# The first wave's weight bytes laid out on chip, the norm's first guess by integer operations, row tiles in another load order, row halves spread over the first steps

## The chip, the cores and the metric

The kernel runs on one core of one Trainium2 chip. The core has five engines that take their own instruction streams: TensorE (PE, matrix products and transposes), VectorE (DVE), ScalarE (ACT), GpSimd (POOL) and SyncE (SP, which here only issues transfers). ACT and POOL can issue transfers as well. The metric is the time of one execution on the device in microseconds, the median of three runs.

## The reference

The input is x, 2048 tokens of 1024 numbers. Three layers follow, each on a layer norm of x without learned scale, and each added to x:

```
x = x + 0.5 * ffn(layernorm(x))
x = x + s4(layernorm(x))          # a long convolution along the 1024 columns, by FFT in the reference
x = x + 0.5 * ffn(layernorm(x))   # the same weights again

ffn(x):  h   = silu(x @ Wg) * (x @ Wu)      # Wg, Wu: 1024 x 2752
         out = h @ Wd                        # Wd: 2752 x 1024
W[k, n] = scale[k // 128, n] * (w4[k, n] - (z4[k // 128, n] + 1))
```

The weights are stored as 4-bit numbers, eight in an int32 word: word row r holds the weight rows 8r to 8r+7. Scales and zero points belong to groups of 128 rows.

## The kernel before

**Tiles.** Tokens are taken in four blocks of 512 (four row tiles of 128 rows each). The kernel makes eight jobs of them, one per block and feed-forward layer, in the order JOBS; job 0 is block 0 in the first layer. A job is `gate_up` and then `down`. `gate_up` goes through eight waves (WAVES): the columns of Wg and Wu in blocks of 128, three blocks of each in waves 0 to 4, two in the others. A wave has eight steps, one per group of 128 input rows (STEPS), so a step of wave 0 takes one weight tile of 128 x 768 and makes 12 products of 128x512: six units (a unit is 128 columns of gate or of up), each with the low part (f16, tile xTl) and the high part (fp32r, tile xTh) of the normalized, transposed activations. Every unit accumulates in a PSUM bank of its own. Because each group has its own scale, the sum is multiplied between steps by the ratio of neighbouring scales (`scaled`, tile rat), on ACT for even units and mostly on DVE for odd ones; the product of the next step into that bank waits for it. After the last group `gated` makes the hidden tile.

**Weights.** For a wave the packed words are fetched (`fetch`), split into bytes by integer operations on DVE (`split`, `signed_bytes`: two shifts, two additions of the zero points, bit flips), copied to int8 planes (`dequantize`, plane j is weight rows j, j+8, ...), and written to a DRAM tensor of bytes, w_q[w] (`keep_bytes`). From there `load_bytes` loads a tile of 128 rows and `make_weights` casts it to fp32r on POOL (in a few steps of job 0 on ACT). `next_weights` runs ahead of the products: at step i it loads tile i+4 and casts tile i+3. The later jobs read the same w_q. The zero points of all waves are unpacked on DVE (`zero_points_in_pieces`: eight pieces zi, then the table ztab), stored to DRAM (z_dram) and read back spread over rows (`fetch_zeros`).

**The start.** `start` is written out by hand. It fetches the first wave's words (raw) and zero words, issues the four row tiles x_0_t of block 0 alternately on SP and ACT (line 1899), and the scales of the first blocks. `first_split` (line 583 on) makes the bytes of wave 0: the zero table z (DVE, line 360), the two shifts, two additions and a flip. In `dequantize_first` odd planes are copied by POOL and even ones by ACT, and 16 of a plane's 128 rows go by a transfer of 12 KB straight into `first_tile`, the weight tile of step 0; the whole planes are written to w_q[0] by four stores (`keep_first`, on POOL, ACT and SP), and the tiles of steps 1 to 7 are loaded from there. `first_moments` makes mean and variance: tile 1 on ACT (two passes), the others on DVE. The factor 1/sqrt(variance) comes from `guess` (a power on POOL, line 205) and Newton steps on DVE (`deviations`). `first_rows` normalizes rows, even tiles on DVE and odd ones on ACT, in pieces of 128, 384 and 512 columns; `first_turn(c)` transposes 128 columns of all four tiles on PE, takes the high part out of PSUM (ACT) and makes the low part (DVE; for c of 3, 5, 7 POOL splits a copy of ACT's). `keep_warm` gives PE transposes that nobody reads.

**Order.** A planner orders each engine's instructions by its own estimates, unless the code pins them: `in_order_of_writing(f, engines...)` ties the instructions of f on these engines behind the last one written there. All of `start` is pinned on ACT, DVE, SP, PE and POOL (STARTING is ACT, DVE and SP). Later work of the start, such as turns 1 to 7, the scales of further blocks, the splits of waves 1 and on, hangs on hooks of `gate_up`: `at(up, s, f)` calls f before the products of step s, and s + 0.5 in their middle. The products of steps 0 to 5 are pinned on PE; the loads of steps 0 to 7 on SP; the casts on POOL are not pinned.

## Time and profile before

| What | us |
|---|---|
| median of three runs (2031.41 to 2032.62) | 2032.05 |
| the profiled execution's own time | 2031.49 |
| its span, first to last instruction | 2029.6 |
| PE busy, share of the span | 2002.4, 99% |
| DVE, ACT, POOL busy | 1628.9, 1415.6, 1371.5 |
| first product of step 0 | 17.85 |
| first product of step 1 | 23.13 |
| first product of step 8 (second wave) | 47.3 |
| granted TensorE clock, mean | 0.999 |

The profile is one execution. A line of its timeline gives start, length, engine (SPq and ACTq are transfers issued by SP and ACT), source line, operation, what is written and read, how many instructions are merged, and in brackets how long the engine idled just before and what ended that. Busy time of PE counts its transposes too, and a busy PE need not be at its peak, so the number of products in a stretch is read beside it.

### The profile page before, as it was taken

The page shows a single profiled execution, that of the slowest core. Times are in us where ns is not written, and L with a number is a line of the kernel's source. Part 1 is how long each engine was busy: PE and PEld are TensorE (multiplying, and loading weights), DVE is VectorE, ACT ScalarE, POOL GpSimd, SP SyncE. Part 2 cuts the span into 40 slices and gives each one's busy share as a digit, 9 for nine tenths or more (in the row PEclk, how much of TensorE's full clock was granted, in tenths as well). Part 3 has the DMA queues.
Part 4 walks back from the last instruction along what each step waited for, and adds up shares of the span by engine and source line. Part 5 has one row for each costly group of instructions (what it writes and reads, how often), then busy time and mean ns, then how long its engine had stood idle before and what let it go on. Part 6 is the DMA issues. An engine that isn't in the chain of part 4 may idle for free.

```text
span 2029.6 us, 29690 instructions
## 1 busy us (share of the span) xinstructions
PE 2002.4 (99%) x9202; PEld 1372.3 (68%) x9202; DVE 1628.9 (80%) x2710; ACT 1415.6 (70%) x2222; POOL 1371.5 (68%) x1772
## 2 busy tenths in 40 slices
PE   7999999999999999999999999999999999999998
PEld 4556766577766677656866578667686676866576
DVE  8988878868888878887778777887878878777776
ACT  7888787747775577777767776764776647767776
POOL 6978768748765577655976578754686637965542
PEclk9999999999999999999999999999999999999999
DMA  5343422343524237311552126242263331651113
GB/s 166 119 130 110 130 80 60 80 103 94 146 62 101 75 77 192 120 29 35 143 162 85 33 50 172 79 93 83 50 161 94 83 92 38 160 189 34 35 36 103
DMA packets 345965, 197.13 MB, mean 97 GB/s; under 512 B 166989, under 2 KB 323670, under 8 KB 345798
## 3 DMA queue, kind: packets, MB, share of 16 engines
q1 hardware_dynamic: 344350, 192.81, 35.1%
q10 hardware_dynamic: 1320, 1.94, 0.3%
q8 instruction: 75, 1.23, 0.3%
q14 instruction: 92, 0.75, 0.1%
q0 software_dynamic: 128, 0.39, 0.1%
HBM read 127.52 MB, written 48.57 MB: 87 GB/s over the span
## 4 chain that ended last, share of the span: by engine, by line
PE 95%; DVE 3%; ACT 1%; POOL 0%; issue 0%; DMA 0%; ACTq 0%; DVEq 0%
PE pg L855 60%; PE po L955 30%; PE pc L1344 3%; PE pb L1344 1%; DVE pg L815 1%; ACT pg L811 0%; DVE po L815 0%; DVE rawd L629 0%; DVE stats L1848 0%; PE pt L239 0%; POOL q L670 0%; DMA raw<-in_L_ffn_up_qweight_dram 0%; DVE rawd L632 0%; DVE r L224 0%; PE po L985 0%
## 5 line engine op out<-in xcount | busy, mean ns | idle before, releaser
L811 ACT ACTIVATE pg<-pg,rat 128x512 f32<-128x512 f32 x1280 | 806.4, 660 | 382.3 <-PE pg L855 378.4
L815 DVE TENSOR_TENSOR pg<-pg,rat 128x512 f32<-128x512 f32 x1128 | 748.5, 692 | 147.1 <-PE pg L855 138.7
L855 PE MATMUL pg<-xTh,w_up 128*128 128x512 f32 x2752 | 844.4, 435 | 1.9 <-DVE pg L815 0.7
L855 PE MATMUL pg<-xTl,w_up 128*128 128x512 f16 x2752 | 707.6, 381 | 2.4 <-DVE pg L815 2.0
L855 PEld LDWEIGHTS pg<-xTh,w_up 128*128 128x128 f32 x2752 | 518.4, 189 | 166.1 <-ACT pg L811 7.2
L788 POOL CAST w_up<-b 128x768 fp32r<-128x768 int8 (+2 forms) x491 | 375.4, 771 | 353.5 <-PE pg L855 257.0
L811 ACT ACTIVATE po<-po,ratd 128x512 f32<-128x512 f32 x669 | 438.0, 662 | 145.5 <-PE po L955 144.9
L955 PE MATMUL po<-hl,w_down 128*128 128x512 f32 x1340 | 525.1, 393 | 2.0 <-DVE po L815 1.8
L955 PE MATMUL po<-hh,w_down 128*128 128x512 f32 x1340 | 520.3, 390 | 0.0
L815 DVE TENSOR_TENSOR po<-po,ratd 128x512 f32<-128x512 f32 x611 | 423.9, 696 | 113.2 <-PE po L955 112.9
L855 PEld LDWEIGHTS <-w_up 128*128 128x128 bf16 x2752 | 226.9, 98 | 339.6 <-issue 154.4
L788 POOL CAST w_down<-bd 128x512 fp32r<-128x512 int8 x352 | 218.2, 623 | 148.5 <-PE po L955 75.5
L955 PEld LDWEIGHTS po<-hl,w_down 128*128 128x128 f32 x1340 | 251.2, 188 | 63.4 <-DVE po L815 7.2
L955 PEld LDWEIGHTS po<-hh,w_down 128*128 128x128 f32 x1340 | 251.6, 188 | 50.9
L897 POOL TENSOR_TENSOR hl<-hf,hh 128x512 fp32r<-128x512 f32 x168 | 217.0, 1292 | 7.0
L896 POOL CAST hh<-hf 128x512 fp32r<-128x512 f32 x168 | 108.5, 646 | 81.2 <-DVE hf L890 62.4
L890 DVE SCALAR_TENSOR_TENSOR hf<-pg,rat,g 128x512 f32<-128x512 f32 x168 | 120.9, 746 | 38.3 <-ACT g L887 32.6
L887 ACT ACTIVATE g<-pg,rat 128x512 f32<-128x512 f32 x168 | 110.0, 687 | 33.9 <-PE pg L855 17.9
L1029 POOL TENSOR_TENSOR x<-x,yr 128x512 f32<-128x512 f32 x52 | 66.8, 1285 | 0.0
L291 POOL TENSOR_TENSOR lo<-x,hi 128x512 f16<-128x512 f32 x48 | 62.0, 1291 | 0.0
L189 DVE BATCH_NORM_STATS2 stats<-x 128x6 f32<-128x512 f32 x88 | 60.0, 682 | 0.0
L289 POOL TENSOR_TENSOR mid<-hi,top 128x512 bf16<-128x512 f32 x48 | 56.0, 1166 | 0.0
(225 smaller groups left out, 1083.3 us busy)
## 6 DMA issues: line engine op xcount, KB each, us to landing
b<-wq SPq DMA_DIRECT2D x319, 96.0 KB
bd<-wdq SPq DMA_DIRECT2D x336, 64.0 KB
x<-in_L_attn_u_dram SPq DMA_DIRECT2D x30, 512.0 KB
yz<-y SPq DMA_DIRECT2D x56, 256.0 KB
yr<-yz SPq DMA_DIRECT2D x56, 256.0 KB
b<-wq SPq DMA_DIRECT2D x128, 64.0 KB
sz<-xn SPq DMA_DIRECT2D x16, 512.0 KB
st<-sz SPq DMA_DIRECT2D x64, 128.0 KB
```

The costliest lines, as they stand in the source:

```text
L291: nc.gpsimd.tensor_tensor(lo[:, own], n[:, own], hi[:, own].bitcast(F32), ALU.subtract)
L788: nc.gpsimd.tensor_copy(t, b)
L811: nc.scalar.activation(dst, src, AF.Copy, scale=sc)
L815: nc.vector.tensor_tensor(dst, src, sc.to_broadcast(list(dst.shape)), ALU.mult)
L855: product = lambda: nc.tensor.matmul(p, weights, (lo, hi)[k][:, g, :], start=(g == 0 and not done), stop=(g == GK - 1 and done), skip_grou ...
L887: nc.scalar.activation(g, pg, AF.Silu, scale=rat[:, 2 * f, GK - 1 :])
L890: nc.vector.scalar_tensor_tensor(hf, pu, last, g, ALU.mult, ALU.mult)
L896: nc.gpsimd.tensor_copy(hi, hf)
L897: nc.gpsimd.tensor_tensor(lo, hf, hi.bitcast(F32), ALU.subtract)
L955: nc.tensor.matmul(ps[c], w[:, bass.ts(c, P)], part, start=(f == 0 and k == 0), stop=(f == NF - 1), skip_group_check=True,)
L1029: nc.gpsimd.tensor_tensor(part, part, rows_back.pop((a, t)), ALU.add)
L1344: nc.tensor.matmul(dst, lhsT, rhs, start=start, stop=stop, skip_group_check=True)
```

## The change

The words of wave 0 are fetched with their row groups interleaved: partition 8r+g holds word row r of group g (rearranged source; the zero words are spread to match). Then the 128 rows of a plane j are, in order, the rows that belong to partitions j, j+8, ... of the eight weight tiles, and one transfer of 96 KB per plane puts them all into `landed`, 128 partitions x 8 tiles x 768 bytes, which takes the place of the loads of steps 0 to 7. `landed` lies in the pool of the y tiles; it is written to w_q[0] in one transfer at step 3 (`keep_landed`). The bytes of wave 1 no longer use that pool: they go to four half tiles with four stores (`keep_half`), their copies are pinned on ACT, and the loads of tiles 8 and 9 and the cast of tile 8 are put off (LATE) to step 5.5, behind these stores.

The zero table of wave 0 goes from DVE to ACT; the zero words of the other waves are fetched on SP instead of ACT. Row tile 1 is issued first, then 2, 0, 3, and DVE takes tiles 2, 0, 3. `first_deviations` replaces power and Newton steps by an integer first guess and two steps on DVE, ten instructions on 128x4 numbers. The scale work of the first blocks comes after all planes and its reciprocal between the first and second row pieces. The high part of turn 0 is taken out half by DVE, half by ACT. Seven zero pieces stay in `start`, the last three calls move to step 0.5; the second row halves (512 columns) move from `start` to steps 1, 1.5 and 2; turns 2 and 3 move by half a step. Step 0 takes all six high products first and then the six low ones. Further hooks of steps 0 to 9 shift by half a step or more, one rescale at step 4 goes from ACT to DVE, and the rescales of steps 0 to 6 are pinned.

```diff
...
             own = slice(GK * SEG * i, GK * SEG * (i + 1))
-            nc.scalar.dma_start(z[own], src.rearrange("g (s n) -> (g s) n", s=SEG))
+            nc.sync.dma_start(z[own], src.rearrange("g (s n) -> (g s) n", s=SEG))
         return z
...
-    def unpacked_zeros_in_pieces(tab, z, zi):
+    def unpacked_zeros_in_pieces(tab, z, zi, on_act=False):
...
             yield
...
+        if on_act:
+            nc.scalar.activation(dst, src, AF.Copy, bias=120.0 * 257, scale=-8.0 * 257)
+        else:
+            nc.vector.tensor_scalar(dst, src, -8.0 * 257, 120.0 * 257, ALU.mult, ALU.add)
...
-    first_tile = bpool.tile([P, width_of(0)], I8, tag="b", name="b_0_0")
+    landed = ypool.tile([P, 4 * TB], F32, tag="y", name="landed").bitcast(I8)[:, : 8 * width_of(0)]
+    landed = landed.rearrange("p (g n) -> p g n", g=GK)
     minus_128 = const.tile([P, 1], F32, tag="minus_128", name="minus_128")
...
         for own, i, lo, hi in columns(w):
-            queues[i].dma_start(raw[:, own], (gate_qw, up_qw)[i][:, lo:hi])
+            src = (gate_qw, up_qw)[i][:, lo:hi]
+            if w == 0:
+                src = src.rearrange("(g r) n -> r g n", g=GK)
+            queues[i].dma_start(raw[:, own], src)
             yield
...
             src = (gate_qz, up_qz)[i][:, lo // 8 : hi // 8]
-            wide = src.unsqueeze(1).to_broadcast([GK, 16, own.stop - own.start])
+            wide = src.unsqueeze(0).to_broadcast([16, GK, own.stop - own.start])
             queue.dma_start(z[:, own], wide)
...
         raw = packed.pop(0)[0]
-        unpacked_zeros(z, zq, zi)
+        unpacked_zeros(z, zq, zi, True)
         nc.vector.tensor_scalar(even, raw, 3, NIBBLES, ALU.logical_shift_left, ALU.bitwise_and)
...
                 nc.scalar.activation(q, view(even, U8), AF.Identity, bias=minus_128)
-            queue = nc.scalar if j == 6 else nc.sync
-            queue.dma_start(first_tile[j:P:8], q[: P // 8])
-
-        def keep(odd, half, queue):
-            rows = w_q[0].rearrange("(r b a two) n -> two b r a n", b=2, a=2, two=2)[odd, half]
-            queue.dma_start(rows, pairs[odd, half].rearrange("p (a n) -> p a n", a=2))
-
-        return dequantize, keep
+            queue = nc.scalar if j in (2, 6) else nc.sync
+            queue.dma_start(landed[j:P:8], q)
+
+        return dequantize
+
+    def keep_landed():
+        nc.sync.dma_start(w_q[0].rearrange("(g p) n -> p g n", p=P), landed)
+
...
         n = width_of(w)
+        if w == 1:
+            if j % 4 < 2:
+                half = t2(f"q_1_{j}").bitcast(I8)[:, : 2 * n]
...
         if w == 1 and j % 2 == 0:
...
...
+    def keep_half(odd, half):
+        rows = w_q[1].rearrange("(r b a two) n -> two b r a n", b=2, a=2, two=2)[odd, half]
+        nc.sync.dma_start(rows, unpacked.pop((1, odd, half)))
...
             s0 = (0, 4, 8 * w - (14 if w < 5 else 15))[min(w, 3) - 1]
-            steps = (0.5, 1, 2.5, 3, 3) if w == 1 else range(6)
+            steps = (1.5, 2, 3, 3.5, 3.5) if w == 1 else (1, 1.5, 2, 3, 4, 5) if w == 2 else range(6)
             in_pieces(at, [(up, s0 + d) for d in steps], lambda w=w: split(w))
-            copies = {1: (3, 3, 3.5, 3.5) + (3.5,) * 4, 2: (3, 3, 4, 4, 5.5, 5.5, 6, 6)}
+            copies = {1: (3.5, 4, 5, 5.5) + (4,) * 4, 2: (3, 3, 4, 4, 5.5, 5.5, 6, 6)}
             copies = copies.get(w, (3, 3, 4, 5, 6, 6, 7, 8))
...
             for k, d in zip(EVEN_FIRST, copies):
-                at(up, s0 + d, lambda w=w, k=k: dequantize(w, k))
-            for odd, o in enumerate({1: (3.5, 3.5), 2: (5.5, 7)}.get(w, (6.5, 9.5))):
+                make = lambda w=w, k=k: dequantize(w, k)
+                make = lambda w=w, k=k, make=make: in_order_of_writing(make, *STARTING[:1] * (w == 1))
+                at(up, s0 + d, make)
+            if w == 1:
+                for odd, half, s in ((0, 0, 4.5), (1, 0, 4.5), (1, 1, 5), (0, 1, 5.5)):
+                    at(up, s, lambda odd=odd, half=half: keep_half(odd, half))
+                at(up, 5.5, late_weights)
+                continue
+            for odd, o in enumerate({2: (5.5, 7)}.get(w, (6.5, 9.5))):
                 at(up, s0 + o, lambda w=w, odd=odd: keep_bytes(w, odd))
...
         j, stage, s = queue[i]
-        if i == 0:
-            loaded[i] = first_tile
+        if i < GK:
+            loaded[i] = landed[:, i, :]
             return
...
             make_weights(k)
-        if i + LOAD < len(queue):
+        if i + LOAD < len(queue) and i + LOAD not in LATE:
             load_bytes(i + LOAD)
-        if i + MAKE < len(queue):
+        if i + MAKE < len(queue) and i + MAKE != LATE[0]:
             make_weights(i + MAKE)
         return made.pop(i)
+
+    LATE = GK, GK + 1
+
+    def late_weights():
+        for i in LATE:
+            load_bytes(i)
+        make_weights(LATE[0])
...
             if j == s == 0:
-                turns = [(1 - k, pos, done) for k, pos, done in turns]
+                turns = [(1 - k, pos, k == 1) for k in range(2) for pos in range(len(order))]
             for i, (k, pos, done) in enumerate(turns):
-                if i == len(order):
+                if i == len(order) // (1 + (j == s == 0)):
                     for hook in hooks.get(s + 0.5, ()):
...
                     if unit == 2 * fs[0 if n == 3 else 1] + 1:
-                        on_act = (j == 0 and n == 3 and g in ((4, 6) if s < 8 else (0, 4, 6)))
+                        on_act = (j == 0 and n == 3 and g in ((6,) if s < 8 else (0, 4, 6)))
                         on_act = on_act or (j < 2 and g % 2 == 0 and (j or n == 2))
...
                     rescale = lambda: scaled(on_act, p, p, rat[:, unit, g : g + 1])
-                    in_order_of_writing(rescale, *STARTING[:2] * (j == s == 0))
+                    in_order_of_writing(rescale, *STARTING[:2] * (j == 0 and s < 7))
                 elif unit == 2 * WIDE:
...
                 rows = {}
-                for s, f in ((0, lambda: fetch_zeros(1)), (1, lambda: fetch(2)), (2, lambda: fetch_zeros(2))):
+                for s, f in ((1, lambda: fetch_zeros(1)), (1, lambda: fetch(2)), (2, lambda: fetch_zeros(2)), (3, keep_landed)):
                     at(up, s, pinned(f, ET.SP))
-                for first_use, s, k0, k1 in ((4, 0, 3, 9), (6, 1, 9, 15), (30, 11, 15, WIDE)):
+                for first_use, s, k0, k1 in ((3, 0, 3, 9), (5.5, 1, 9, 15), (30, 11, 15, WIDE)):
                     load = lambda k0=k0, k1=k1: rows.update({k0: scale_rows(k0, k1)})
                     at(up, s, lambda load=load: in_order_of_writing(load, ET.SP))
-                    steps = [(up, first_use + i / 2) for i in range(4)]
+                    late = {3: 1.5, 9: 0.5}.get(k0, 0)
+                    steps = [(up, first_use + i / 2 + late * (i > 1)) for i in range(4)]
                     in_pieces(at, steps, lambda k0=k0, k1=k1: scales_in_pieces(k0, k1, rows.pop(k0)))
...
                     more = lambda c=c: first_turn(c)
-                    at(up, {1: 0.5, 2: 0.5, 4: 2.5}.get(c, c - 2), pinned(more, *STARTING, ET.PE))
+                    at(up, {1: 0.5, 2: 1, 3: 1.5, 4: 2.5}.get(c, c - 2), pinned(more, *STARTING, ET.PE))
+                for _ in range(3):
+                    at(up, 0.5, pinned(lambda: next(points, None), ET.Activation, ET.DVE))
+                for t, s in ((0, 1.5), (1, 1), (2, 2), (3, 1.5)):
+                    more = lambda t=t: first_rows(t, 512, HID)
+                    at(up, s, pinned(more, *STARTING))
                 first_weights(up, dn, at)
...
         nc.scalar.activation(scratch, x[0][1], AF.Square, bias=mean, scale=-1.0, accum_out=squares)
-        for t in (0, 2, 3):
+        for t in (2, 0, 3):
             for i in range(2):
...
         return mv, scratch
+
+    def first_deviations(mv):
+
+        tiny = lambda a: small.tile([P, NT], F32, tag=a, name=f"{a}_0_1")
+        ve, r, e = tiny("ve"), tiny("r"), tiny("e")
+        nc.vector.tensor_scalar(ve, mv[:, :, 1], EPS, (256 / (3 * LIFT)) ** 2, ALU.add, ALU.mult)
+        bits = r.bitcast(I32)
+        nc.vector.tensor_scalar(bits, ve.bitcast(I32), 1, -1, ALU.logical_shift_right, ALU.bitwise_and)
+        nc.vector.tensor_scalar(bits, bits, -1.0, float(0x5F3759DF - 2**31), ALU.mult, ALU.add)
+        nc.vector.tensor_tensor(e, r, r, ALU.mult)
+        nc.vector.tensor_tensor(e, e, ve, ALU.mult)
+        nc.vector.scalar_tensor_tensor(r, e, -3.0, r, ALU.add, ALU.mult)
+        nc.vector.tensor_tensor(e, r, r, ALU.mult)
+        nc.vector.tensor_tensor(e, e, ve, ALU.mult)
+        nc.vector.scalar_tensor_tensor(e, e, -40.0 / 3, e, ALU.add, ALU.mult)
+        nc.vector.scalar_tensor_tensor(r, e, 80.0, r, ALU.add, ALU.mult)
+        for t in range(NT):
+            ln[0, t] = (mv[:, t, 0:1], r[:, t : t + 1], 1)
+        return r
...
         ps = bank(f"pt_0_1_{c}")
-        for t in range(NT):
+        for t in (0, 2, 1, 3):
             src = first[t, c // 4][:, bass.ts(c % 4, P)]
             nc.tensor.transpose(ps[:, bass.ts(t, P)], src, ident)
-        if c not in (3, 5, 7):
+        if c == 0:
+            for i, copy in enumerate((nc.vector.tensor_copy, nc.scalar.copy)):
+                view = lambda a: a.rearrange("p (t two n) -> p two t n", two=2, n=P)[:, i]
+                copy(view(hi), view(ps))
+            nc.vector.tensor_tensor(lo, ps, hi.bitcast(F32), ALU.subtract)
+        elif c not in (3, 5, 7):
             nc.scalar.copy(hi, ps)
...
         fetch(0, (nc.sync, nc.scalar))
-        for t, src in enumerate(rows_of(u, 0)):
-            (nc.sync, nc.scalar)[t % 2].dma_start(x[0][t], src)
+        for t, queue in ((1, nc.sync), (2, nc.scalar), (0, nc.sync), (3, nc.scalar)):
+            queue.dma_start(x[0][t], rows_of(u, 0)[t])
         nc.gpsimd.memset(minus_128, -128.0)
...
         zeros_down = zero_words(1)
-        dequantize_first, keep_first = first_split(zq)
+        dequantize_first = first_split(zq)
         second = fetch_in_pieces(1)
-        for j in (1, 3, 5):
+        mv, scratch = first_moments()
+        for j in (1, 0, 3, 2, 5, 7, 4, 6):
             dequantize_first(j)
-        next(second)
-        dequantize_first(7)
-        mv, scratch = first_moments()
-        dequantize_first(0)
+        for _ in second:
+            pass
         first_scales = scales_in_pieces(0, 3, srow)
         next(first_scales)
-        dequantize_first(2)
         next(first_scales)
-        guess(0, 1, mv, LIFT)
-        for _ in range(2):
-            keep_first(1, _, nc.gpsimd)
-        dequantize_first(4)
-        dequantize_first(6)
-        keep_first(0, 1, nc.scalar)
-        keep_first(0, 0, nc.sync)
-        next(second)
-        for _ in first_scales:
-            pass
         keep_warm(10, scratch)
...
         bias = small.tile([P, NT], F32, tag="bias", name="bias")
-        r = deviations(0, 1)
+        r = first_deviations(mv)
+        points = zero_points_in_pieces(0, zeros)
         nc.vector.scalar_tensor_tensor(bias, mv[:, :, 0], -1.0, r, ALU.mult, ALU.mult)
...
             first_rows(t, 0, P)
-        for t in (0, 1, 2):
+        for _ in first_scales:
+            pass
+        for t in (0, 2, 1):
             first_rows(t, P, 512)
-        points = zero_points_in_pieces(0, zeros)
-        for _ in range(4):
+        first_turn(0)
+        first_rows(3, P, 512)
+        for _ in range(7):
             next(points)
-        first_turn(0)
-        for _ in range(5):
-            next(points)
-        first_rows(3, P, 512)
-        for t in range(NT):
-            first_rows(t, 512, HID)
-        for _ in points:
-            pass
         keep_warm(6)
-        return zeros_down
-
-    zeros_down = in_order_of_writing(start, *STARTING, ET.PE, ET.Pool)
+        return zeros_down, points
+
+    zeros_down, points = in_order_of_writing(start, *STARTING, ET.PE, ET.Pool)
     x.pop(0)
...
```

More of the change, by code (lines that the diff above doesn't have):

```diff
@@ L359, in unpacked_zeros_in_pieces @@
             yield
-        nc.vector.tensor_scalar(
-            tab.bitcast(U16).rearrange("p (n k) -> p n k", k=2),
-            zi.unsqueeze(2).to_broadcast([p, 8 * n, 2]),
-            -8.0 * 257,
-            120.0 * 257,
-            ALU.mult,
-            ALU.add,
-        )
+        dst = tab.bitcast(U16).rearrange("p (n k) -> p n k", k=2)
+        src = zi.unsqueeze(2).to_broadcast([p, 8 * n, 2])
+        if on_act:
+            nc.scalar.activation(dst, src, AF.Copy, bias=120.0 * 257, scale=-8.0 * 257)
+        else:
+            nc.vector.tensor_scalar(dst, src, -8.0 * 257, 120.0 * 257, ALU.mult, ALU.add)
     def zero_points(which, z):
@@ L662, in dequantize @@
         n = width_of(w)
-        if w not in unpacked:
-            q = ypool.tile([P, 4 * TB], F32, tag="y", name=f"q_{w}").bitcast(I8)[:, : 8 * n]
-            unpacked[w] = q.rearrange("p (two a n) -> p two a n", two=2, a=4)
-        q, src = unpacked[w][:, j % 2, j // 2, :], packed[w][j % 2][:, j // 2, :]
+        src = packed[w][j % 2][:, j // 2, :]
+        if w == 1:
+            if j % 4 < 2:
+                half = t2(f"q_1_{j}").bitcast(I8)[:, : 2 * n]
+                unpacked[1, j % 2, j // 4] = half.rearrange("p (a n) -> p a n", a=2)
+            q = unpacked[1, j % 2, j // 4][:, j // 2 % 2, :]
+        else:
+            if w not in unpacked:
+                q = ypool.tile([P, 4 * TB], F32, tag="y", name=f"q_{w}").bitcast(I8)[:, : 8 * n]
+                unpacked[w] = q.rearrange("p (two a n) -> p two a n", two=2, a=4)
+            q = unpacked[w][:, j % 2, j // 2, :]
         if w == 1 and j % 2 == 0:
@@ L670, in dequantize @@
             nc.gpsimd.tensor_copy(q, src)
-        if j == 7:
+        if j == (6 if w == 1 else 7):
             packed.pop(w)
```

## The prediction

> **What bounds the kernel now.** First the page: engine shares and the chain that ended last.
>
> ```profile
> span 2029.6 us, 29690 instructions
> PE 2002.4 (99%) x9202; PEld 1372.3 (68%) x9202; DVE 1628.9 (80%) x2710; ACT 1415.6 (70%) x2222; POOL 1371.5 (68%) x1772
> ...
> PE 95%; DVE 3%; ACT 1%; POOL 0%; issue 0%; DMA 0%; ACTq 0%; DVEq 0%
> ```
>
> TensorE is the bound; 27.2 us (2029.6 - 2002.4) is all that it ever idles. The change touches only the start, so the second view is the busy time of each engine in stretches cut at the first product (17.85), the second step (23.13) and the eighth (44.60).
>
> ```profile
> 0.00:17.85 17.85, 5.83 (x34) 5.00 (x34) 13.40 (x38) 9.37 (x16) 9.77 (x22) 1.00 0.57 189
> 17.85:23.13 5.28, 4.39 (x24) 2.97 (x25) 4.48 (x15) 4.67 (x8) 0.92 (x2) 1.00 0.63 202
> 23.13:44.60 21.47, 20.39 (x102) 12.13 (x101) 18.80 (x29) 17.63 (x30) 18.56 (x24) 1.00 0.41 126
> 20.10:44.60 24.50, 22.53 (x113) 13.48 (x112) 21.06 (x32) 20.43 (x35) 19.48 (x25) 1.00 0.44 134
> ```
>
> Columns: stretch, PE, PEld, DVE, ACT, POOL busy, then clock 1.00 and DMA. In 23.13 to 44.60 three helpers are each over 80% busy. After it the chain has 31.95 us for 140 products, 0.228 each, so a step of 12 costs 2.7. Seven steps at 2.7 (18.9), seven turns of activations at 0.44 (3.1) and two groups of scale turns at 0.47 (0.9) make 22.9 us; 17.85 to 44.60 is 26.75. So 3.85 us can be won there, and whatever the first product comes earlier.
>
> Third, the timeline of the start.
>
> ```profile
> 8.55 1.06 ACT L1844 ACTIVATE scratch<-x 128x1024 f32<-128x1024 f32 x1 [3.67 <-DMA x<-in_L_attn_u_dram]
> 13.46 1.04 POOL L205 TENSOR_TENSOR r<-ve,minus_half 128x4 f32<-128x4 f32 x1 [0.42 <-DVE ve L203]
> 14.45 1.72 POOL L613 DMA_DIRECT2D wq<-q  x2
> 16.74 1.35 DVE L351 TENSOR_SCALAR zi<-zq 128x43 int32<-128x43 int32 x4
> 16.94 0.81 POOL L788 CAST w_up<-b 128x768 fp32r<-128x768 int8 x1
> 17.15 0.56 ACT L1880 CAST xTh<-pt 128x512 fp32r<-128x512 f32 x1
> 17.85 0.93 PE L855 MATMUL pg<-xTh,w_up 128*128 128x512 f32 x3 [0.17 <-POOL w_up L788]
> 20.11 1.24 ACT L811 ACTIVATE pg<-pg,rat 128x512 f32<-128x512 f32 x2 [0.38 <-DVE xn L1865]
> 22.21 1.60 POOL L788 CAST w_up<-b 128x768 fp32r<-128x768 int8 x2 [4.45 <-DMA b<-wq]
> 22.64 0.66 PE L1878 MATMUL pt<-ident,xn 128*128 128x128 f32 x4 [0.89 <-DVE xTl L1881]
> 23.10 1.12 DVE L625 TENSOR_SCALAR even<-raw 128x768 int32<-128x768 int32 x1
> ```
>
> POOL stood 4.45 us for the second tile's bytes, yet PE at 22.64 was held by DVE's low half. Both waits end at 23.0 to 23.1, so taking only the bytes' trip away gives nothing.
>
> **The change part by part.** Times are single records of this trace.
>
> *Row tiles.* They land in order of issue at 7.08, 8.52, 9.82 and 10.52. Tile 1 goes first, so ACT's 2.4 us of moments begin at 7.1 instead of 8.55. DVE reads tile 2 (8.52) at 8.95, tile 0 (9.82) at 10.30, tile 3 (10.52) at 11.70: no wait. DVE's line, from the packed words (5.31) through the statistics to 13.2, is the longer one, so by itself this gives 0; it lets ACT finish its even planes by 13.5 (14.4 before), with one more DMA issue (0.54) among them.
>
> *Zero table on ACT.* On DVE it ran 4.39 to 5.35, inside the wait for the words that ended at 5.31: gain 0. On ACT the shape is not shown: between 1.06 (128x1024) and 1.6 (that times 1.5) from 4.87, done by 5.9 to 6.5; DVE needs it at 6.52. I take 0; end +0.1.
>
> *Planes.* Eight transfers of 12 KB become 96 KB; four stores (1.72 us of POOL's issue, 0.73 of ACT's, 0.58 of SP's), three loads and their wait go. SP's issues stay near 0.5 each; its order meets planes ready at 9.6, 10.35, 10.4, 11.2, 11.9, 12.7, so nothing queues long, and the two zero-word DMAs that move to SP fall in its gap before 9.65. A 96 KB load took 2.45 (19.71 to 22.16); the last plane, issued at 13.5 on ACT, lands at 16.0. POOL can cast five tiles straight on, 4 to 5 us earlier than now.
>
> *First guess.* From the variance (13.21) to the bias (15.38) was 2.17, with POOL's 1.04 inside. Now ten dependent DVE instructions at the 0.20 to 0.26 that the Newton steps show: 2.0 to 2.6. I take 2.1, so 0; ends -0.15 and +0.4.
>
> *First product.* The reciprocal (0.45) sat beside POOL's power and now lies between DVE's row pieces. DVE: bias at 15.3, two pieces at 0.25, reciprocal 0.45, two at 0.39, then its half of the first high part, between 0.3 and 0.56 (ACT's whole one): 0.4. High part at 17.5 (17.70 before). POOL: ratios 0.37 and 0.43 after the reciprocal at 16.35, cast 0.82: 17.97 (17.755 before). First product at 18.0, +0.1; if the cast goes before the ratios, 17.5, -0.3.
>
> *First step.* The second row halves leave it. ACT's first rescale stood at 20.11. Now: three products to 18.7, turn 0.44, ACT's copy to 19.8, DVE's low half to 20.45, the last zero piece and the table (0.7) to 21.2, ACT's store of the table, whose issue stands ahead of the rescales, to 21.6. So ACT starts its rescales 1.5 later than before, DVE at 21.2 against 20.43. The seven zero pieces in front take 0.65 (0.09 apart where POOL is idle) and fit DVE's gap from 18.2 to 19.8.
>
> *To the eighth step.* Both helpers' lists: ACT has 20 rescales at 0.57 (11.4), 6 copies at 0.58 (3.5), 2 row halves at 0.71 (1.4), 2 scale copies (0.5), 4 planes at 0.83 (3.3): 20.1, from 21.6 to 41.7. DVE has 19 rescales at 0.60 (11.4), 3 low halves at 0.61 (1.8), 2 row halves at 0.46 (0.9), the next splits (0.56, 0.56, 0.96, 0.96, 0.57 and 0.56, 0.56, 0.96: 5.7), a reciprocal 0.75: 20.6, from 21.2 to 41.8. PE alone would be there at 40.9. With no wait 41.8, -2.8. ACT idled 24.5 - 20.4 = 4.1 in the same stretch before; with all of that, 45.9, +1.3. Two idles have lost their cause: the 1.26 us before 42.99, where POOL's plane copies held back the scales, whose reciprocal now comes 1.5 steps later, and some 0.5 around 23 to 26 that hung on the second tile. 2.3 remain: 44.1, -0.5.
>
> *Second wave's bytes.* The next load is late here if anything is. Tile 8's cast waits for four stores, whose last plane ACT makes in the middle of step 5. From that plane's end: store 2.95 (38.96 to 41.9), load 2.45, cast 0.82, issues 0.2: 6.4. Two and a half steps with a turn and scale turns are 7.2 to 7.7, less about 1 of queue on ACT: slack -0.2 to +0.3. I take 0; end +1. The 768 KB kept at step 3 on SP goes ahead of these stores; the same bytes in four stores took 5.2 (14.45 to 19.65), so it ends before them: 0, and +2 if not.
>
> *After.* From 44.6 the list of work is the same and shifts as a whole: 0, give or take 0.5.
>
> Sum: -0.5. The profiled execution itself took 2031.49 (span 2029.6 and 1.89 around it) and would take 2031.0; it lies 0.56 under the median 2032.05, so the predicted median is 2031.5.
>
> **A rule against the change.** The rows first: one zero piece, issued at 16.74 as POOL's cast began, took 1.079 us where the seven others took 0.19, and the 0.56 shift at 23.10 took 1.12 under casts. At 500.7 two DVE instructions on rows, under four POOL casts, took turns with them, one for one.
>
> [...]
>
> **The rivals.**
> *The lock (slower).* In 17.75 to 22.21, when DVE unpacked zeros, POOL idled; now it casts there. If one zero piece passes per cast, five casts at 0.8 let DVE go at 22.4 instead of 18.85; low half to 23.0, table to 23.8, store to 24.2: first rescale 24.2, not 21.6. That is +2.6 on the sum, less 0.6 of blocking that the later splits no longer meet (the 0.56 at 23.10): +1.5 in all, 2033.5; from +0.5 to +4 (if all idle stays). It decides once three of the seven pieces take over 0.5 each. Against it: small pieces overlap and may pass together.
> *Second wave late (slower).* If tile 8's cast ends after step 7, every step from there waits: +1 to +5, 2035. For it: the slack above. Against: before, the cast ended at 45.98 for a use at 47.3.
> *All stalls gone (faster).* First product at 17.6 and PE unhindered: 17.6 + 22.9 = 40.5, -4.1, 2028; up to -2.8 if the lists bind without idling. Against: three helpers over 80% busy.
> *The bytes were hidden anyway.* The low half at 22.64 says so; then the same idle stays, +1.3 at most; it is the upper end of my case.
>
> **How the numbers follow.** 0.2% is 4.1 us, about what a measurement of this kernel can tell from no change. My case, -2.8 to +1.3 (2029.2 to 2033.4): 0.45. Lock 0.30, second wave late 0.10, all stalls gone 0.15. Faster by over 4.1: half of the last (0.07) and 0.06 for later stretches moving: 0.13. Slower: a third of the lock (0.10), most of the second wave (0.06), 0.03 for the rest: 0.19. Within: 0.68. Range: 2028.2, below which half of the all-gone case lies, to 2036.0, above which lie a tenth of chance of the lock and the second wave.
>
> **What would show it.** ACT's moments at 7.1; no stores of the first wave before step 3; casts two to five right behind the first; POOL without a power; first product at 17.5 to 18.1; first ACT rescale at 21.6 (24.2: the lock, with zero pieces of 0.8); eighth step at 44.1; tile 8's cast ended before it is used. Wrong if DVE's row pieces also stand behind casts before the first product, or if the order on POOL, which only the planner sets, puts ratios or later turns behind five casts.

## The result and the profile after

The changed kernel takes 2035.76 us (median of 14, 2033.57 to 2037.45), the kernel before, run beside it, 2031.99 (2030.86 to 2033.0): a ratio of 1.0019 with a 95% interval of 1.0011 to 1.0026. So it is slower, by about 3.8 us. Its profiled execution took 2035.14, 3.65 more than that of before (2031.49); the two profiles are compared below. The page of the changed kernel:

```profile
span 2033.3 us, 29687 instructions
...
PE 2003.5 (99%) x9202; PEld 1373.6 (68%) x9202; DVE 1631.6 (80%) x2716; ACT 1416.6 (70%) x2222; POOL 1368.9 (67%) x1769
```

PE is busy for 1.1 us more and idle for 29.8 us instead of 27.2. Step starts (first product of each step) show where:

| step | before | after | shift |
|---|---|---|---|
| first | 17.85 | 18.13 | +0.28 |
| second | 23.13 | 24.31 | +1.18 |
| third | 26.48 | 29.06 | +2.58 |
| fourth | 30.10 | 34.33 | +4.23 |
| eighth | 44.61 | 47.65 | +3.04 |
| ninth | 47.30 | 51.46 | +4.16 |
| seventeenth | 69.15 | 73.05 | +3.90 |
| sixty-fourth | 184.10 | 187.77 | +3.67 |

Everything is lost in the first nine steps, and the rest only carries it on. Busy time by stretch of the changed kernel, cut at its first product, second and eighth step (columns as in the prediction):

```profile
0.00:18.13 18.13, 5.86 (x33) 5.06 (x34) 12.65 (x41) 11.02 (x17) 7.04 (x20) 1.00 0.64 211
18.13:24.31 6.18, 3.85 (x21) 2.55 (x22) 6.15 (x14) 1.71 (x4) 3.87 (x5) 1.00 0.05 18
24.31:47.65 23.34, 21.95 (x104) 13.68 (x104) 21.61 (x32) 20.07 (x34) 16.22 (x21) 0.93 0.39 124
```

In the second stretch DVE is busy for 6.15 of 6.18 us (4.48 of 5.28 before), with fewer instructions, and ACT for only 1.71. In the third the granted clock is 0.93, where it was 1.00. The timeline of that second stretch says why DVE has no time:

```profile
17.26 3.92 POOL L808 CAST w_up<-landed 128x768 fp32r<-128x768 int8 x5
...
17.96 0.69 DVE L1935 TENSOR_TENSOR xTl<-pt,xTh 128x512 f16<-128x512 f32 x1 [0.44 <-ACT xTh L1934]
...
18.57 2.93 DVE L351 TENSOR_SCALAR zi<-zq 128x43 int32<-128x43 int32 x7
...
21.40 0.68 DVE L1938 TENSOR_TENSOR xTl<-pt,xTh 128x512 f16<-128x512 f32 x1
...
22.00 0.57 DVE L351 TENSOR_SCALAR zi<-zq 128x43 int32<-128x43 int32 x1
22.60 0.52 DVE L365 TENSOR_SCALAR ztab<-zi 128x688 uint16<-128x688 int32 x1
...
23.15 0.34 ACTq L378 DMA_DIRECT2D z_dram<-ztab  x1
23.59 1.81 ACT L838 ACTIVATE pg<-pg,rat 128x512 f32<-128x512 f32 x3 [3.44 <-DVE ztab L365]
24.31 1.24 PE L882 MATMUL pg<-xTl,w_up 128*128 128x512 f16 x3 [2.32 <-ACT pg L838]
```

Five casts run without a gap, as the change meant them to. Beside them seven zero pieces of 43 elements take 2.93 us: four at 0.19 to 0.35 and three at 0.88, one for each of three casts. DVE's low half of the second turn waits behind the pieces, and behind it the eighth piece and the table. ACT's queue stands 3.44 us at the store of the table, with three rescales behind it. PE, which needs those rescales, stands 2.32.

Then comes a second loss. Clock and busy time of PE in three stretches of 3.41 us around that wait:

```profile
21.13:24.54 3.41, 1.09 (x8) 0.71 (x7) 3.38 (x10) 0.95 (x2) 0.87 (x2) 1.00 0.14 51
24.54:27.96 3.42, 3.42 (x12) 2.57 (x11) 2.39 (x5) 3.42 (x7) 0.00 (x0) 0.50 0.15 46
27.96:31.37 3.41, 3.41 (x22) 2.12 (x21) 2.75 (x5) 2.94 (x5) 1.93 (x3) 1.00 0.81 239
```

PE was busy for 1.09 of 3.41 us, and its clock was halved for the next 3.42: 12 matmuls (8 products and 4 transposes) where the stretch after it has 22 (12 and 10). In the third and fourth step DVE then lost more turns to POOL, as these lines of its timeline show:

```profile
30.03 0.99 DVE L1917 TENSOR_SCALAR xn<-x,mv,r 128x512 f32<-128x512 f32 x1
30.94 1.64 DVE L627 TENSOR_SCALAR raw<-raw 128x768 int32<-128x768 int32 x1
...
37.34 1.52 DVE L634 TENSOR_SCALAR raw<-raw 128x1536 uint16<-128x1536 uint16 x1
```

A row half took 0.99 (0.54 in the kernel before, at 19.52), a shift 1.64 and a bit flip 1.52 (0.55 for the shift at 27.61 and for the flip at 55.1). The ninth step waited 0.95 for the cast of its tile.

### The profile page after: what moved, and what is told of

Read it like the earlier page. It is cut to its first block, busy times and chain, and to the rows that moved or that the text cites. A ratio compares the mean times of both kernels' runs of the same rounds, so it can differ in the third digit from the quotient of the medians.

```text
span 2033.3 us, 29687 instructions
## 1 busy us (share of the span) xinstructions
PE 2003.5 (99%) x9202; PEld 1373.6 (68%) x9202; DVE 1631.6 (80%) x2716; ACT 1416.6 (70%) x2222; POOL 1368.9 (67%) x1769
## 3 DMA queue, kind: packets, MB, share of 16 engines
q8 instruction: 75, 1.23, 0.2%
## 4 chain that ended last, share of the span: by engine, by line
PE 95%; DVE 3%; ACT 1%; issue 0%; DMA 0%; POOL 0%; ACTq 0%; DVEq 0%
PE pg L882 60%; PE po L982 30%; PE pc L1371 3%; PE pb L1371 1%; DVE pg L842 1%; ACT pg L838 0%; DVE po L842 0%; DVE rawd L631 0%; DMA raw<-in_L_ffn_up_qweight_dram 0%; DVE stats L1881 0%; PE pt L239 0%; DVE zi L351 0%; DVE rawd L634 0%; PE po L1012 0%; DVE r L224 0%
## 5 line engine op out<-in xcount | busy, mean ns | idle before, releaser
L808 POOL CAST w_up<-b 128x768 fp32r<-128x768 int8 (+2 forms) x483 | 368.7, 769 | 348.5 <-PE pg L882 257.4
```

The lines of the kernel that those rows point to most:

```text
L808: nc.gpsimd.tensor_copy(t, b)
```

## The experiments

Each kernel's ratio is to the kernel before, timed beside it (medians of 2030.87 to 2031.99), with a 95% interval in brackets. A profile is one execution, and often one of the faster ones: its rows account for that execution, and not for the whole of a median.

**The bytes alone, and one tile alone.** The kernel before, its tiles of the first steps cast from the bytes of the first tile, which lie on the chip at once. The right weights of steps 1 to 7, and their loads, are left out. For the second kernel `i < 2` stands in place of `i < GK`:

```diff
-        if i == 0:
+        if i < GK:
             loaded[i] = first_tile
```

> The kernel before, with one edit: the weight tiles of steps 1 to 7 are cast from the same bytes as that of step 0, so they wait for no trip through DRAM (this leaves the right weights of these steps out of the computation). Theory that the bytes were hidden, plus the lock: POOL casts at 17.7 to 21 instead of 22.2 to 25.6, but DVE's last zero pieces, table and two row halves (18.6 to 20.5) now stand behind casts, so the second step begins 0.3 to 1.5 us later than 23.13, and the kernel is between 1 us faster (POOL's relief later) and 1.5 us slower. Theory that the trip was the stall: the second step at 22.3 or earlier, and 1.5 to 3 us faster than before.

> The kernel before, with the second tile alone cast from the bytes of the first (its weights are wrong in that step), so two casts follow one another at 17.1 instead of five. If a row piece of DVE is starved as long as casts follow without a gap (4.5 with five casts): it takes 2.0 to 2.3 with two, ending at 18.7, and the second step starts at 24.5 to 25 instead of 27.18 with five; eighth step 45 to 46, time 2032 to 2033. If DVE and POOL take turns one for one: the piece takes 1.2 at most, the second step starts at 23.1 as before and the time is 2031.5.

With all tiles: 2035.2 against 2031.48, ratio 1.0020 (1.0010 to 1.0030). The early bytes by themselves cost as much as the whole change. Its timeline:

```profile
15.77 5.44 DVE L1865 TENSOR_SCALAR xn<-x,mv,r 128x128 f32<-128x128 f32 x4
...
17.09 3.90 POOL L788 CAST w_up<-b 128x768 fp32r<-128x768 int8 x5
...
22.22 1.22 PE L855 MATMUL pg<-xTl,w_up 128*128 128x512 f16 x3 [3.29 <-DVE xTl L1881]
```

The last of the four row pieces (128x384) begins at 16.68, before the casts, while POOL works on the scales, and takes 4.54 us; the piece of the same shape ahead of it takes 0.47. It ends 0.2 after the fifth cast, at the first gap in POOL's work since 16.5. The casts keep their 0.81 to 0.82. So it isn't one turn for one. With two casts in a row (2032.7 against 2031.0, ratio 1.0008, 0.9998 to 1.0017):

```profile
16.68 2.13 DVE L351 TENSOR_SCALAR zi<-zq 128x43 int32<-128x43 int32 x4
...
16.88 1.59 POOL L788 CAST w_up<-b 128x768 fp32r<-128x768 int8 x2
...
18.70 0.68 DVE L1881 TENSOR_TENSOR xTl<-pt,xTh 128x512 f16<-128x512 f32 x1
```

Here the first of four zero pieces is the one that waits, 1.87, until the second cast is over. The second step starts at 23.86, less late than the 24.5 that I had expected: the row piece was through before the casts began. By the profiles what is lost grows with the casts in a row: the second step starts at 23.13 before, 23.86 with two and 27.19 with five. The times of the two kernels lie 1.0008 and 1.0020 over before, with intervals that overlap.

**The zero pieces, the store.** Seven pieces between the dependent instructions of the guess, before any cast; and, in another kernel, the table's store issued by SP (with the calls at step 0.5 pinned there as well):

```diff
         nc.vector.tensor_tensor(e, r, r, ALU.mult)
+        next(between, None)
...
-        for _ in range(7):
-            next(points)
```
```diff
-... else (z_dram, SEG, nc.scalar)
+... else (z_dram, SEG, nc.sync)
```

> The changed kernel, with one edit: seven of the eight zero pieces leave their place behind the first low half and stand between the dependent instructions of the norm's first guess on DVE, where POOL makes no cast. Lock theory (three pieces of 0.88 us behind POOL's casts hold the second low half, the table and with it ACT's store): the pieces take 0.2 each, the first product comes up to 0.6 later (18.1 to 18.7), ACT's first rescale goes from 23.6 to about 21.8 and the second step from 24.3 to 22.5 to 22.9; the kernel is 1.5 to 2.0 us faster than the changed one (about 2034.0). Rival theory (the row halves moved into steps 1 and 2 overload ACT and DVE, whenever these start): the second step begins earlier, but the fourth (34.3) moves by less than 0.7 and the time by less than 0.7.

> The changed kernel, with one edit: the store of the zero table is issued by SP instead of ACT, so that ACT's rescales do not stand behind an issue that waits for DVE's table. Lock theory with its second half (the loss reaches PE through ACT's queue): DVE's pieces stay at 0.88, but ACT's idle 3.44 us before 23.6 shrinks to about 1, its first rescale comes at 20.7 to 21.0, and though DVE's first rescale stays at 23.0 the backlog on ACT in steps 1 and 2 is 2.5 us smaller: 1.0 to 2.5 us faster than the changed kernel. If DVE alone carries the loss: second step within 0.5 of 24.3 and under 0.7 us gained.

Early pieces: each takes 0.2, the second low half begins at 20.38 in place of 21.40, the first ACT rescale is at 22.45 and the second step at 23.16, as before the change. But the median is 2035.37, ratio 1.0022 (1.0013 to 1.0032): no gain. In the profiled execution, the fastest of ten (2033.48), PE still stands 0.99, 1.18 and 0.94 at 22.2, 36.0 and 48.1, and the fourth step is at 31.32 (30.10 before); what the slower executions lose isn't shown. Store on SP, by its timeline:

```profile
18.59 2.93 DVE L351 TENSOR_SCALAR zi<-zq 128x43 int32<-128x43 int32 x7
...
20.58 1.82 ACT L838 ACTIVATE pg<-pg,rat 128x512 f32<-128x512 f32 x3 [0.41 <-PE pg L882]
```

The pieces are as slow as ever, but ACT rescales 3 us sooner, and the second step is at 22.24. The time is 2034.25, ratio 1.0015 (1.0006 to 1.0025): off ACT's queue the store leaves the kernel 2.8 above the one before in place of 3.8, a difference that the intervals don't separate. Neither edit alone brings the time back.

**The casts held back.** POOL reads one element before it casts tiles two to five: of the second low half, or (with the store on SP) of the table; in a third kernel, with the pieces early, the store on SP and the order of copies that is tried next, the cast of each tile from the second to the eighth comes behind the low half of the turn before its own. The first kernel's edit, in part:

```diff
...
+    def held_weights():
+        nc.gpsimd.tensor_copy(t, pieces[0][1][:1, 1, :1])
+        for k in range(1, MAKE + 1):
+            make_weights(k)
```

> The changed kernel, with its bytes as early as before, but POOL reads one element of the second turn's low half before it casts the second tile, so casts two to five can't run beside the zero pieces. If the lock between DVE's unpacking and POOL's run of casts is what slows the change: zero pieces of 0.2 to 0.35 instead of 0.88, the second low half at 19.8 to 20.4 instead of 21.40, casts two to five at 20.5 to 24, second step at 23.1 to 23.4 instead of 24.31, eighth step at 45 to 46 instead of 47.65, time 2032 to 2033.5. If the row halves and the store in steps 0 to 2 are what slows it, and the lock only fills idle time: the eighth step stays at 47.4 to 47.8 and the time at 2035 to 2036.

> The changed kernel with casts two to five held until DVE has the table of zero points (one element of it read by POOL), and the table's store on SP, so that neither the lock nor the store stands before ACT's first rescale. Lock and store together as the cause: zero pieces 0.2 to 0.35, first rescale on ACT at 20.2 to 20.7, second step at 22.2 to 22.6, eighth step near the 44.1 of the prediction, time 2030.8 to 2032, no slower than the kernel before. If the row halves in steps 1 and 2 cost as much as they save: eighth step at 45 to 46.5, time 2032.5 to 2034.

> The three edits together (zero pieces early, store on SP, third-wave copies in order), and casts two to eight no longer back to back: POOL reads one element of the low half of a turn before it casts the tile after next to that turn's (tile c+1 behind turn c), so casts come one per turn. If runs of casts without a gap are what the chip punishes: DVE instructions lengthened by under 2 us in all between 15 and 52 us, no PE gap over 0.8 before the ninth step, eighth step at 42.5 to 43.5, and a spread of executions as narrow as that of the kernel before (3 us or less); median 2029 to 2030.5. If the waits put on POOL cost what the lock cost: a cast late for its step (PE waiting for POOL at a step's start), eighth step 44 to 46, median 2031 to 2033.

Held behind the low half: 2034.48 against 2031.0, ratio 1.0015 (1.0005 to 1.0024). Its timeline:

```profile
17.21 0.82 POOL L808 CAST w_up<-landed 128x768 fp32r<-128x768 int8 x1
...
18.57 0.74 DVE L351 TENSOR_SCALAR zi<-zq 128x43 int32<-128x43 int32 x7
...
20.14 0.69 DVE L1945 TENSOR_TENSOR xTl<-pt,xTh 128x512 f16<-128x512 f32 x1 [0.83 <-ACT xTh L1944]
...
20.98 1.23 DVE L365 TENSOR_SCALAR ztab<-zi 128x688 uint16<-128x688 int32 x1
21.02 4.19 POOL L808 CAST w_up<-landed 128x768 fp32r<-128x768 int8 x5
...
23.40 0.95 PE L888 MATMUL pg<-xTl,w_up 128*128 128x512 f16 x3 [1.47 <-ACT pg L844]
```

Without casts beside them the seven pieces take 0.74 in place of 2.93, so the casts are what stretched them; the table, now under a cast, takes 1.23 in place of 0.52. The profiled eighth step is at 45.50 in place of 47.65. Behind the table, with the store on SP: first rescale 20.66, second step 22.70, as expected. Then comes, by its timeline,

```profile
28.00 1.08 DVE L1925 TENSOR_SCALAR xn<-x,mv,r 128x512 f32<-128x512 f32 x1
...
29.13 0.55 PE L1938 MATMUL pt<-ident,xn 128*128 128x128 f32 x3 [1.21 <-DVE xn L1925]
```

the stretching of a row half that the change moved to step 2, from 0.54 to 1.08, and PE waits for it. What runs beside it here is POOL's split of a turn (27.53, 1.26), not a cast. Eighth step 44.89, 2034.07, ratio 1.0013 (1.0004 to 1.0023). Paced: second step 21.87, the same wait of 1.2 at 28.0, eighth step 44.95, 2034.97, ratio 1.0016 (1.0007 to 1.0025), and no wait of PE over 0.5 between the second and the ninth step was ended by a cast. My expectation for it failed both ways: casts no longer ran back to back, none was late for PE, and yet POOL's work met other instructions of DVE. Held casts are not lost casts: they, or the work that they push back, land on something else.

**Third-wave copies behind the casts on POOL**, so that tile 8's cast is not queued behind one:

```diff
-..., *STARTING[:1] * (w == 1))
+..., *STARTING[:1] * (w == 1), *[ET.Pool] * (w == 2))
```

> The changed kernel, with one edit: the third wave's first copies are pinned on POOL behind the casts written before them, so the cast of tile 8 (at 50.58, behind a copy at 49.81) comes first. Second-wave theory: the copy's 0.77 us on POOL is what PE idles 0.95 for at 50.5; the ninth step begins at 50.6 to 50.8 instead of 51.46, and the kernel is 0.7 to 0.9 us faster than the changed one (about 2035.0). If instead the bytes themselves are late (loaded at 49.3), the ninth step moves by less than 0.3.

The changed kernel's timeline around tile 8:

```profile
49.32 0.54 POOL L431 TENSOR_TENSOR rat<-s_gu,safe 128x84 f32<-128x84 f32 x1 [1.69 <-DVE safe L427]
...
49.81 0.82 POOL L679 COPY q<-even 128x768 int8<-128x768 int8 x1
...
50.58 1.60 POOL L808 CAST w_up<-b 128x768 fp32r<-128x768 int8 x2
...
51.46 0.82 PE L882 MATMUL pg<-xTl,w_up 128*128 128x512 f16 x3 [0.95 <-POOL w_up L808]
```

With the copy behind, the cast is at 49.98 and the ninth step at 50.85, 0.61 sooner; by the seventeenth step it is 73.13 against 73.05, and the time is 2036.2, ratio 1.0027 (1.0016 to 1.0037). The ninth step's wait for its cast exists, and taking it away gains nothing that shows here.

**The row halves back in the start; the power back.** The halves are all written in the start again; or POOL's power and the Newton steps are the first guess again, first ahead of the plane copies, then behind them.

```diff
-        r = first_deviations(mv)
+        r = deviations(0, 1)
```

> The changed kernel with all four second row halves back in the start, as before the change. If bytes that come early are what slows the change, through the lock: no better, ACT's first rescale at 23.5 to 25, second step 24 to 26, time 2034.5 to 2036. If it is the row halves spread over steps 1 to 2 that overload ACT and DVE there: fourth step at 31 to 32 instead of 34.33, eighth at 45 to 46, time 2032.5 to 2033.5.

> The changed kernel with POOL's power and the Newton steps as the first guess, as before. The prediction has the two guesses equal: variance to bias 2.0 to 2.3, first product 18.0 to 18.3, the time within 0.5 of the changed kernel's. If the guess is worth something by itself: first product 0.3 to 0.5 later and the time as much longer.

> The changed kernel with POOL's power and the Newton steps as the first guess, the power behind the four plane copies on POOL. By the prediction's sum (2.17 against 2.1) nothing changes: variance to bias 2.0 to 2.4, first product 17.9 to 18.5, time within 0.7 of the changed kernel's 2035.8. If the integer guess saves POOL's turn for the scales: first product 0.4 to 1 later, time as much longer.

Rows back: 2035.54, ratio 1.0019 (1.0010 to 1.0029), the pieces at 0.84 to 0.90 again, fourth step 34.95: the spread of the halves is not the cause. The power ahead of the copies took 2039.21 (1.0040, 1.0025 to 1.0055), but told of the queue and not of the guess: the power waits for the variance until 13.79, four plane copies follow it, and the Newton steps, 0.16 to 0.23 in the kernel with the power behind the copies, take 0.73 to 0.77 beside them. The timeline of this kernel:

```profile
13.79 1.02 POOL L205 TENSOR_TENSOR r<-ve,minus_half 128x4 f32<-128x4 f32 x1 [12.42 <-DVE ve L203]
14.78 3.13 POOL L607 COPY q<-raw 128x768 int8<-128x768 int8 x4
...
15.65 0.73 DVE L220 TENSOR_TENSOR e<-e,ve 128x4 f32<-128x4 f32 x1
16.42 0.73 DVE L222 SCALAR_TENSOR_TENSOR f<-e 128x4 f32<-128x4 f32 x1
```

With the power behind the copies: variance to bias 2.23 (2.02 with integers, 2.17 before), first product 18.53, 2036.39 against 2031.83, ratio 1.0023 (1.0013 to 1.0033). The interval holds the changed kernel's 1.0019: the 0.2 us that the guess saves in the profile is nothing that these times show.

**A second profiled execution of the changed kernel.**

> The changed kernel once more, for a second profiled execution. If the lock is won by chance: the lengthened instructions are others, the eighth step lies at 45.5 to 49 and not at 47.65, while the start up to 17.3 us agrees within 0.1. If each execution loses the same: eighth step 47.5 to 47.8, the same instructions lengthened.

Its start is later (bias at 16.17 in place of 15.47), so the first product is at 18.83; the pieces take the same within 0.01. Its timeline, and its busy time in two stretches of 3.41 us:

```profile
19.28 2.93 DVE L351 TENSOR_SCALAR zi<-zq 128x43 int32<-128x43 int32 x7
...
25.02 0.95 PE L882 MATMUL pg<-xTl,w_up 128*128 128x512 f16 x3 [2.33 <-ACT pg L838]
```
```profile
20.18:23.60 3.42, 2.51 (x14) 1.39 (x13) 3.39 (x9) 0.59 (x1) 2.53 (x4) 1.00 0.00 0
23.60:27.01 3.41, 1.99 (x11) 1.40 (x11) 2.37 (x5) 2.71 (x5) 0.00 (x0) 1.00 0.15 54
```

So in these two executions the same pieces wait. The clock differs: PE stood 2.33 us, against 2.32 in the first, but the clock stayed at 1.00; in the two stretches, which share the wait, PE was busy for 2.51 and 1.99. Why the clock fell in the one execution and not in the other is not shown. Against the first profile it gains 1.2 from first product to eighth step (28.3 against 29.5), and 0.4 of that is left at the sixty-fourth. It took 2036.3, so the clock is not what makes the changed kernel slow.

**Three edits together**: pieces early, store on SP, third-wave copies behind; then ACT's two row halves back in the start besides.

> The changed kernel with three edits at once: seven zero pieces between the instructions of the first guess, the table's store on SP, the third wave's plane copies in written order on POOL. The casts still run back to back from 17.3. If the lock costs only through the zero pieces and the store: first rescale at 20.5, second step at 22.3, eighth step 44 to 44.6, ninth at 47, time 2031 to 2032. If the run of casts also holds whatever DVE instruction is next (the low halves, the rescales, the row halves): gaps of about 1 return at steps 2 to 4, eighth step 45 to 46, time 2033 to 2034.5.

> The version with zero pieces early, store on SP and third-wave copies in order, once more. If its executions differ by when the row tiles land: the first product differs from 18.42 by as much as the time differs from 2029.73. If they differ by which DVE instructions lose to the casts: first product within 0.1, eighth step later than 43.09 by most of the difference. If by a later stretch: eighth step within 0.3 and the shift appears behind it.

> The same version a third time, with the same three expectations.

> The version with zero pieces early, store on SP and third-wave copies in order, in five rounds. If the median of timed executions follows the profiled ones (2029.7 to 2031.2): ratio 0.999 to 1.000. If timed executions lose something that no profiled one shows: 2032 to 2033, ratio 1.0005 to 1.001.

> The same version with ACT's two second row halves back in the start, where ACT waits for DVE anyway. If the row halves in steps 1 and 2 cost: the second to eighth steps come 0.3 to 1 earlier (eighth at 42 to 42.8) and the time is as much shorter. If ACT's halves now delay its copy of the second turn (19.8): second step 0.5 to 1.2 later than 22.1, time 0 to 1 longer.

In the first profile of the three edits the first steps run without a long wait. Its timeline:

```profile
17.55 3.92 POOL L808 CAST w_up<-landed 128x768 fp32r<-128x768 int8 x5
...
20.49 0.69 DVE L1945 TENSOR_TENSOR xTl<-pt,xTh 128x512 f16<-128x512 f32 x1 [1.55 <-ACT xTh L1944]
20.86 1.82 ACT L838 ACTIVATE pg<-pg,rat 128x512 f32<-128x512 f32 x3 [0.40 <-PE pg L882]
```

Beside the five casts DVE has the turn's copy and low halves, which read PSUM, and of the rest only the eighth piece (0.43). No PE gap up to the ninth step exceeds 0.55; second step 22.12, eighth 43.08; it took 2029.73. Three more profiles of it took 2031.17, 2030.47 and 2032.04, with the eighth step at 42.76 to 42.98. In all four the sixty-fourth step begins 1.0 to 1.5 before that of the kernel before (182.57 to 183.12 against 184.10). But the medians are 2032.33 against 2031.0 (ratio 1.0008, 0.9999 to 1.0018) and 2032.02 against 2030.87 (1.0011, 1.0002 to 1.0020): two thirds of the loss is given back, and the kernel before still isn't beaten. Of the 21 executions, ten with a mean granted clock of 0.999 took 2029.7 to 2032.0, eleven with 0.998 took 2032.0 to 2037.4. None of the four profiles is of the second kind, so what those executions lose, and whether the clock falls in their start, stays open. The mean alone doesn't say it: the profile with the casts held behind the low half has 0.998 too, and its clock is 1.00 throughout from 18 to 48 us. A halved clock also stands at the end: 0.50 over the last 5.18 us of the kernel before (from 2024.39) and the last 5.17 of the changed one (from 2028.16), where PE is busy for 0.00. With ACT's halves back: fourth step 31.03 in place of 30.15, a row half and a shift stretched again (1.00 and 1.17 at 27.2 and 28.1), 2032.51, ratio 1.0011 (1.0002 to 1.0020), no gain.

## Why the prediction was wrong

The step that failed is *First step*: "The seven zero pieces in front take 0.65 (0.09 apart where POOL is idle) and fit DVE's gap from 18.2 to 19.8." They took 2.9, from 18.57 to 21.4. POOL was not idle there; the paragraph on planes had put five casts in that place. A row with a cast beside the piece was at hand (1.079 at 16.74), stood in the prediction among the rows against the change, and was left to the rival. All behind it follows: the low half 21.4 for 19.8, first rescale on ACT 23.6 for 21.6, second step 24.31. That the time still lies inside the stated range (up to 2036.0) is owed to the rivals that set its upper end; the sum, -0.5, pointed the other way from the +3.8 measured.

The lock rival had the pattern (one piece for each cast), the place and its condition (three pieces over 0.5: three at 0.88), and a first rescale at 24.2 against the 23.6 measured. Its price of 1.5 was too small against 3.8 (its end of +4 is near): it took 0.6 off for splits that would no longer be stretched, while a row half (0.99), a shift (1.64) and a flip (1.52) were stretched in the third and fourth step, and it knew nothing of the clock, worth 0.4 by the two profiles. It also took one piece per cast as the worst, where the bytes alone show an instruction that waits for all of five.

Of the other steps: first product 18.13 (18.0 predicted); row tiles 0, ACT's moments at 6.6; the guess 0, with 2.02 for 2.1 and nothing to see in the time with the power behind the copies; the zero table on ACT 1.47, so the addition behind it moved by 0.24, where I had +0.1 at most; 0.17 of that was there at the first shift, which waits for the words. Second wave's bytes: a wait of 0.95 at the ninth step, inside the end of +1, and of no worth by the seventeenth. *To the eighth step* gave 44.1 with the first rescale at 21.6; the three edits together, with the first rescale at 20.9 and one zero piece beside the casts, reached 42.8 to 43.1. So the list of work is not contradicted; the durations in it were at fault, since DVE's changed with what POOL ran beside them (the seven pieces 2.93 with casts, 0.74 without).

What stays open is the last third of the loss, 1.2 to 1.3 us with the three edits. The order of the row tiles, the store at step 3, the late loads of tiles 8 and 9 and the new order in step 0 were not tried by themselves.

"The bytes were hidden anyway" fell with the bytes alone: put early into the kernel before, they are not neutral but cost as much as the whole change.

## What to carry to other kernels

A transfer that keeps an engine waiting may also be what keeps it out of another's way: before bytes are brought forward, list what the engine freed by them will run beside. Price an instruction by a row in which the same neighbour is running, and where a queue of one engine gets no gap, price the other's instruction by the whole queue (here 4.54 us through five casts for a row piece, 0.47 for the one ahead of it). Look then at who stands behind the stretched instruction in order (here a store in ACT's queue, 3.44 us), and at PE's clock behind the wait (0.50 for 3.42 us in the first profile, 1.00 in the second).

## What the runs showed of the hardware

- A DVE instruction can lose to several POOL instructions in a row: 4.54 us through five casts at 0.77 from start to start, with the bytes alone. The 43-element pieces beside casts passed one for each cast in the changed kernel (three at 0.88), and with one tile early one of them waited for two casts (1.87). What decides between the two is not shown.
- Not all of DVE is hit: its rescales and low halves, which read PSUM, took 0.674 to 0.700 in all 51 records between 15 and 52 us of the kernels before and after, 15 of them with a weight cast beside. What was stretched worked on SBUF: a row piece (4.54 for 0.47), zero pieces (0.88 for 0.19), a shift (1.64 for 0.55), the table (1.23 for 0.52), the subtraction of zeros (1.25 at 51.74, 0.94 at 36.36).
- PE's clock was 0.50 for 3.41 to 3.42 us after a stretch of 3.41 in which PE was busy for 1.09 us (the changed kernel), 0.25 (the bytes alone) and 1.39 (the row halves back). It stayed at 1.00 after stretches of 3.41 with 1.94 (the casts held behind the low half), 1.99 and 2.51 (the second execution of the changed kernel) and 2.52 (the kernel before). PE's wait before the second step was 2.32 us in the first execution of the changed kernel, where the clock fell, and 2.33 in the second, where it didn't.
